# Shared-expert linear factors taken into the last but one half batch, unbroken last subtractions, and biases behind the last span chain, in a perceiver layer

## Chip, cores and metric

The kernel runs on one core of one Trainium2 chip, as one launch. The metric is the device time in microseconds (us) of one execution; lower is better. All arithmetic is float32.

## What is computed

There are 32 batches of 64 tokens with 256 features, and a context of 1601 rows of 256 features for each batch. Three residual steps follow each other, each on a layer norm of x:

```python
# 1. cross-attention, 16 heads of 16
q, k, v = split(ln(x) @ wq.T + bq), split(ctx @ wk.T + bk), split(ctx @ wv.T + bv)
x = x + merge(softmax(q @ k.T / 4, mask) @ v) @ wo.T + bo
# 2. span attention among the 64 tokens: two numbers per head and token
span = heads(ln(x) @ W_span.T)
mean, soft = sigmoid(span[..., 0]) * 64, softplus(span[..., 1])
x = x + merge(softmax(-soft * (pos - mean)**2) @ heads(ln(x) @ W_val.T)) @ W_out.T
# 3. feed-forward: one shared expert, and two of eight experts chosen by the token's index
xf = ln(x)
shared = (silu(xf @ sw1 + sb1) * (xf @ sw3 + sb3)) @ sw2 + sb2
routed = sum(gelu(xf @ w1[e] + b1[e]) @ w2[e] + b2[e] for e in two_experts(token)) / 2
x = x + (shared + routed) / 2
```

## The kernel before

**Engines.** PE is TensorE, DVE VectorE, ACT ScalarE, POOL GpSimd; SP issues nearly all loads and stores. PE, DVE, ACT and POOL run their instructions in the order in which the program writes them between `order.enter_context` (L629) and `order.close()` (L749). Outside that stretch, and for SP's loads and stores throughout, a planner puts the instructions in order by the times that it estimates. PE's results lie in PSUM; six banks of 128 x 512 are shared by most matmuls of the attention part (`mm_bank`, L94), and a bank is used again when its reader is done.

**Half batches.** `halves` (L388) has 64 entries: batch b, and c for the first or last eight heads. The work of half batch n is written in four groups of key blocks (`GROUPS`, L33). While half batch n is normalised, the scores of n+1 are made: `scores` (L461, matmul L469) with the mask added by DVE (L478), running maxima on DVE (L499) begun by a copy on ACT (`first_maxima`, L490). Maxima are turned (L506), reduced (L513), spread over rows (L521) and copied (L525). `less_maxima` (L528) subtracts them from four pairs of heads, on POOL for n < 63 and on DVE for the last n (all at L530); `exponentials` (L534, L535) is ACT's. `values` (L537, L545) multiplies with v. In between, PE projects the keys and values of the next batch (L434, L450); for the last batch there is no next one, so half batches 62 and 63 have none of that.

**Steps between the groups.** Each half batch has four stretches, 4n to 4n+3. `agenda` (L595) holds generators by stretch and `run` (L597) lets each take a step, written into the order at that place. `finish_steps` (L603) ends a batch: a copy (L608), a matmul (L611), a reciprocal (L615) and a product (L618). After every second batch `span_steps` (L206) follows for a tile of 128 tokens, some 17 stretches long: output projection (L210), residual (L213), statistics, L184 on POOL (a power, for the norm's scale), L190 and L191, turn (L198), copy (L220), span matmul (L224) and values (L236), copy of the span (L229) on DVE and of the values (L242) on ACT, absolute value (L250) and exponential (L251) on ACT, a run of small DVE operations (L265 to L281), then on [128, 16, 64]: POOL subtracts (L286), ACT squares (L290), POOL scales (L291), DVE finds the least (L294), POOL subtracts (L295), ACT exponentiates (L297), DVE sums (L299) and inverts (L300), POOL scales (L301); PE turns (L309), ACT copies (L311), PE multiplies (L319), ACT copies (L325), PE multiplies (L329), DVE adds (L332), SP stores the tile to `x_kept` (L334), and after another norm and turn DVE copies it to `xfT` (L340). There are 16 tiles; tile 14 is under way in half batches 60 to 63, tile 15 after the last half batch.

**Shared expert.** Its first layer is cut into 16 units: four quarters of the tokens by four chunks of 128 hidden features. `unit(u)` makes both products (L575) in two PSUM banks; `gate()` applies Silu with its bias on ACT (L590) and adds the other bias and multiplies on DVE (L591). Quarter 3, units 12 to 15, needs tile 15. The results lie in parts of `prob`, the tile of the probabilities, that are free by then (`region`, L558). Units 0 to 2 are made and gated in half batch 62, unit 3 is made and gated and unit 4 made in half batch 63, the others while the last tile's span steps run, by the two tables `begin` (L737) and `gated` (L738), and quarter 3 at the end.

**Experts.** After `order.close()` come the weight loads (L761), the load of the second biases (L773), the doubling of `sw2` on POOL (L775), the biases of the eight classes of tokens on POOL (L780, L784, L787), and for each class a load of its rows of `x_kept` (L796) to which POOL adds the bias (L797). Then for each of eight classes PE makes two experts' hidden layers (L808), ACT applies gelu (L815), PE sums shared and routed outputs (L826), DVE scales and adds the rows (L828) and SP stores (L829).

Of the kernel before, what the change touches and what calls it, by code (L numbers as in the profile page):

```python
# [15 lines left out]
F32 = mybir.dt.float32  # L16
U8 = mybir.dt.uint8
AF = mybir.ActivationFunctionType
# [4 lines left out]
P = 128  # L23
# [53 lines left out]
def perceiver_kernel(ctx: ExitStack, tc: tile.TileContext, a: dict[str, bass.AP], out: bass.AP):  # L77
# [83 lines left out]

    neghalf = const.tile([P, 1], F32, name="neghalf")
# [43 lines left out]
    def span_steps(t: int, oT):  # L206
# [21 lines left out]
        span = span_pool.tile([P, H, 2], F32, tag="span", name=f"span_{t}")  # L228
        nc.vector.tensor_copy(span.rearrange("p h k -> p (h k)"), psp[:, : 2 * H])  # L229

# [18 lines left out]
        z = span_pool.tile([P, H, 2], F32, tag="z", name=f"z_{t}")  # L249
        nc.scalar.activation(z, span, AF.Abs)  # L250
# [315 lines left out]
    waiting: deque = deque()  # L566

    def unit(u: int):
        quarter, hc = divmod(u, NHC)
        slot = slice(quarter * QL, (quarter + 1) * QL)  # L570
        pair = []
        for name, w in (("p1", sw1), ("p3", sw3)):
            ps = mm_bank(f"{name}_{u}")
            for c in range(2):
                nc.tensor.matmul(  # L575
                    ps, lhsT=w[:, c, hc * P : (hc + 1) * P], rhs=xfT[:, c, :, slot],
                    start=(c == 0), stop=(c == 1),
                )
            pair.append(ps)
        waiting.append((u, *pair))  # L580

    def gate():
        u, p1, p3 = waiting.popleft()
        quarter, hc = divmod(u, NHC)
        act = gated_at(1, 2)
        if u > 2:
            act = spare[:, 0, (4 + u % 2) * E * QL : (5 + u % 2) * E * QL]
            act = act.rearrange("p (r i) -> p r i", r=E)
        p1, p3 = (ps.rearrange("p (r i) -> p r i", r=E) for ps in (p1, p3))
        nc.scalar.activation(act, p1, AF.Silu, bias=cols[:, B_S1 + hc : B_S1 + hc + 1])  # L590
        nc.vector.scalar_tensor_tensor(  # L591
            gated_at(quarter, hc), p3, cols[:, B_S3 + hc : B_S3 + hc + 1], act, ALU.add, ALU.mult
        )
# [67 lines left out]
    for n, (b, c) in enumerate(halves):  # L661
# [12 lines left out]
        for g in range(len(GROUPS)):  # L674
            if waiting and n < last:
                gate()
            if g == 0:
                turned = []
                if n < last:

                    def turn():
                        turned.extend(turned_maxima(n))
                        return turned

                    scores(n + 1, g, BETWEEN[g], turn)
                else:
                    turned = turned_maxima(n)
                    maxima_of_rows(*turned)
            elif n < last:
                scores(n + 1, g, BETWEEN[g])  # L690
            if g == 0:
                project(project_keys, c, 0)
                m = maxima_along_rows(turned[1])
                if n == last:
                    unit(3)
# [6 lines left out]
            elif g == 1:  # L702
                project(project_keys, c, 1)
                project(project_values, 3 * c)
            elif g == 2:
                project(project_keys, c, 2)
                if c:
                    project(project_values, 4)
            else:
                project(project_keys, c, 3)  # L710
                for u in range(5 if c else 1, 7 if c else 3):
                    project(project_values, u)

            less_maxima(n, g, m, nc.vector if n == last else nc.gpsimd)
            run(4 * n + g)
            if n == last - 1 and g < 3:
                unit(g)
            if n == last and g == 1:
                gate()
                unit(4)  # L720
            if g == 0 and n < last:
                first_maxima(n + 1)
            if g:
                exponentials(n, g - 1)
        if n < last:
            for k in BETWEEN[-1]:
                maximum(n + 1, k)
    exponentials(last, 3)
    values(last, 0)
    values(last, 1)  # L730
    stretch = 4 * last + 4
    finish = finish_steps(B - 1, stretch)
    next(finish)
    agenda[stretch].append(finish)


    begin = {1: 5, 4: 6, 7: 7, 9: 8, 10: 9, 12: 10, 16: 11}  # L737
    gated = {1: 1, 4: 1, 7: 1, 9: 1, 10: 1, 12: 1, 14: 1}  # L738
    for s in range(19):
        run(stretch + s)  # L740
        for _ in range(gated.get(s, 0)):
            gate()
        if s in begin:
            unit(begin[s])
# [3 lines left out]
    gate()  # L748
    order.close()  # L749
# [22 lines left out]
    b2row = ffn.tile([P, E + 1, D], F32, name="b2row")  # L772
    nc.sync.dma_start(out=b2row, in_=a["b2"].partition_broadcast(P))  # L773

    nc.gpsimd.tensor_tensor(sw2, sw2, sw2, ALU.add)  # L775


    brow = spare[:, 2, 4 * D : (4 + E) * D].rearrange("p (r d) -> p r d", r=E)
    for r in range(E):
        nc.gpsimd.tensor_tensor(  # L780
            brow[:, r, :], b2row[:, expert_of(0, r), :], b2row[:, expert_of(1, r), :], ALU.add
        )
    for _ in range(2):
        nc.gpsimd.tensor_tensor(  # L784
# [112 lines left out]
```

## Time and profile before

| what | value |
|---|---|
| median of 3 runs | 1655.0 us (1652.92 to 1655.36) |
| profiled execution, its own time | 1654.66 us |
| its span, first to last instruction | 1652.9 us |
| mean granted TensorE clock | 0.993 |
| PE busy (share of the span) | 1572.0 us (95%) |
| weight loads on PE busy | 1182.3 us (72%) |
| DVE busy | 1288.4 us (78%) |
| ACT busy | 921.0 us (56%) |
| POOL busy | 1120.8 us (68%) |

The page's second part cuts the span into 40 slices of 41 us. PE stands at nine tenths in nearly all; two slices near the end show 7 and 6, and there the granted clock (PEclk) has its one 7. Most of the program is the same pattern repeated 64 times, which the change doesn't touch but for one small operation per tile; what it does touch lies between 1449.8 us, where half batch 62 begins, and 1566 us, where the routed experts begin. The timeline (instructions in order of time) and the chain of waits (the work that ended last) over that window, and a table of busy times by stretches, are the views to read. In the timeline each row has the start, the duration, the engine, the line and what it writes from what; a number in brackets is the idle time of the engine just before, with what ended it.

### The profile page before, as it was taken

How to read it: one execution, taken by the hardware profiler on the slowest of the kernel's cores; microseconds unless marked ns; L12 is line 12 of the kernel's file. 1: busy time of each engine (PE TensorE's matmuls, PEld its weight loads, DVE VectorE, ACT ScalarE, POOL GpSimd, SP SyncE). 2: the span in 40 equal slices, each digit the busy share in tenths (PEclk: the TensorE clock that was granted, in tenths of full speed). 3: DMA queues.
4: the chain of work that ended last, by engine and by line, in shares of the span. 5: the costliest groups of instructions: out<-in, count | busy, mean ns of one | idle time of the engine just before them, and what ended most of it. 6: DMA issues, size and time to landing. Idle time of an engine off the chain costs nothing.

```text
span 1652.9 us, 55724 instructions
## 1 busy us (share of the span) xinstructions
PE 1572.0 (95%) x25128; PEld 1182.3 (72%) x25128; DVE 1288.4 (78%) x2619; ACT 921.0 (56%) x1279; POOL 1120.8 (68%) x410
## 2 busy tenths in 40 slices
PE   8999999999999999999999999999999999979699
PEld 5777777777777777777777777777777777745388
DVE  4888988888888978888888889888888889785100
ACT  3555656556656556565665656565666565566211
POOL 0777767777686867687686877677776869653600
PEclk9999999999999999999999999999999999999799
DMA  5111111111111111111111111111111111003100
GB/s 174 54 41 30 42 40 33 39 42 49 42 42 48 29 40 34 41 39 48 42 42 49 42 36 36 39 40 39 42 48 42 42 45 30 31 15 109 55 23 29
DMA packets 52045, 73.67 MB, mean 45 GB/s; under 512 B 3812, under 2 KB 51040, under 8 KB 51680
## 3 DMA queue, kind: packets, MB, share of 16 engines
q1 hardware_dynamic: 50992, 69.32, 14.4%
q8 instruction: 197, 3.23, 0.8%
q10 hardware_dynamic: 816, 0.79, 0.1%
q14 instruction: 40, 0.33, 0.1%
HBM read 65.90 MB, written 4.19 MB: 42 GB/s over the span
## 4 chain that ended last, share of the span: by engine, by line
PE 57%; DVE 38%; issue 2%; POOL 1%; ACT 1%; DMA 0%; ACTq 0%; DVEq 0%; POOLq 0%
DVE prob L478 13%; DVE mrun L499 13%; PE pk L434 13%; PE pv L450 13%; PE pvs L545 9%; PE psc L469 8%; PE py L826 3%; DVE rin L615 3%; PE p L575 2%; PE pm L506 2%; PE ph L808 2%; PE pb L521 1%; DVE mrun L279 1%; DVE least L294 1%; PE pval L236 1%
## 5 line engine op out<-in xcount | busy, mean ns | idle before, releaser
L530 POOL TENSOR_TENSOR prob<-prob,mb 124x1664 f32<-124x1664 f32 x252 | 935.3, 3730 | 326.7 <-ACT mb L525 326.7
L478 DVE TENSOR_TENSOR prob<-psc,madd 124x384 f32<-124x384 f32 (+1 forms) x1024 | 582.1, 581 | 183.4 <-PE psc L469 183.4
L499 DVE TENSOR_TENSOR mrun<-prob,mrun 124x512 f32<-124x512 f32 x704 | 483.1, 686 | 7.2 <-ACT mrun L491 4.3
L434 PE MATMUL pk<-ct,wkT_sb 128*128 128x372 f32 (+2 forms) x1024 | 407.8, 521 | 14.3 <-DMA wkT_sb<-in_wkT 5.6
L535 ACT ACTIVATE prob<-prob 124x1664 f32<-124x1664 f32 x256 | 399.6, 1587 | 1.5 <-POOL prob L530 1.0
L450 PE MATMUL pv<-wvT_sb,ct 128*124 128x256 f32 (+1 forms) x1664 | 384.6, 379 | 0.0
L450 PEld LDWEIGHTS pv<-wvT_sb,ct 128*124 128x124 f32 (+1 forms) x1664 | 309.9, 186 | 77.3 <-DVE prob L478 2.4
L469 PE MATMUL psc<-qbd,kT 32*124 32x128 f32 x6656 | 294.6, 286 | 30.6 <-DVE prob L478 26.0
L438 ACT ACTIVATE kT<-pk,cols 128x372 f32<-128x372 f32 (+2 forms) x256 | 152.1, 594 | 292.4 <-PE pk L434 292.0
L469 PEld LDWEIGHTS psc<-qbd,kT 32*124 32x124 f32 x6656 | 232.5, 181 | 104.3 <-DVE prob L478 48.1
L434 PEld LDWEIGHTS pk<-ct,wkT_sb 128*128 128x128 f32 x1024 | 174.2, 190 | 118.7 <-issue 29.4
L456 ACT COPY v<-pv 124x512 f32<-124x512 f32 (+1 forms) x224 | 124.7, 557 | 215.2 <-PE pv L450 213.8
L545 PE MATMUL pvs<-prob,v 124*17 124x64 f32 x13312 | 211.3, 219 | 1.8 <-ACT prob L535 1.8
L545 PEld LDWEIGHTS pvs<-prob,v 124*17 124x17 f32 x13312 | 188.8, 98 | 27.5 <-issue 25.2
L828 DVE SCALAR_TENSOR_TENSOR ot<-py,prob 128x256 f32<-128x256 f32 x16 | 6.8, 424 | 76.9 <-PE py L826 76.9
L615 DVE RECIPROCAL rin<-pr 128x256 f32<-128x256 f32 x32 | 55.9, 1745 | 6.3 <-PE pr L611 6.3
L575 PE MATMUL p<-xfT,sw_sb 128*128 128x512 f32 x128 | 59.7, 619 | 0.7 <-DVE xfT L340 0.4
L521 PEld LDWEIGHTS pb<-cst,mc 128*124 128x124 f32 x256 | 29.8, 135 | 35.8 <-DVE mc L513 30.1
L506 PE MATMUL pm<-cst,mx 124*128 124x124 f32 x256 | 40.7, 282 | 10.4 <-DVE mx L499 9.4
L575 PEld LDWEIGHTS p<-xfT,sw_sb 128*128 128x128 f32 x128 | 25.0, 200 | 30.1 <-issue 27.1
L499 DVE TENSOR_TENSOR mx<-prob,mrun 124x512 f32<-124x512 f32 x64 | 43.9, 686 | 2.2
L815 ACT ACTIVATE hT<-ph,cols 128x256 f32<-128x256 f32 x32 | 13.4, 471 | 57.4 <-PE ph L808 57.4
(123 smaller groups left out, 1235.0 us busy)
## 6 DMA issues: line engine op xcount, KB each, us to landing
ct<-in_ctxT SPq DMA_DIRECT2D x64, 372.0 KB, 3.2
ct<-in_ctxT SPq DMA_DIRECT2D x32, 496.0 KB, 3.5
ct<-in_ctxT SPq DMA_DIRECT2D x32, 361.0 KB, 3.1
w<-in_w SPq DMA_DIRECT2D x16, 256.0 KB, 4.8
x<-in_x SPq DMA_DIRECT2D x16, 128.0 KB, 2.0
x_kept<-x SPq DMA_DIRECT2D x16, 128.0 KB, 1.7
prob<-x_kept SPq DMA_DIRECT2D x8, 256.0 KB, 6.0
out<-ot SPq DMA_DIRECT2D x16, 128.0 KB, 1.9
```

The costliest lines, as they stand in the source:

```text
L434: nc.tensor.matmul(ps[:, :kn], lhsT=wkT[:, i, c * P : (c + 1) * P], rhs=cts[b][g][:, i, :kn], start=(i == 0), stop=(i == 1),)
L438: nc.scalar.activation(kTs[c][:, k0 : k0 + kn], ps[:, :kn], AF.Identity, bias=cols[:, B_K + c : B_K + c + 1])
L450: nc.tensor.matmul(ps[:kn, n * D : (n + 1) * D], lhsT=cts[b][g][:, i, k0 : k0 + kn], rhs=wvT[:, i, :], start=(i == 0), stop=(i == 1),)
L456: nc.scalar.copy(vs[b % 2][:kn, 2 * u : 2 * u + n, :, :DK], ps[:kn, : n * D].rearrange("p (n h d) -> p n h d", n=n, d=DK),)
L469: nc.tensor.matmul(ps[:CHUNK, k * P : (k + 1) * P], lhsT=kTs[c][32 * j : 32 * j + 32, at : at + CHUNK], rhs=qbd[b // 2][32 * j : 32 * j + ...
L478: nc.vector.tensor_tensor(pair_of(n, j)[:, c0 : c0 + nb, :].rearrange("p k (e q) -> p k e q", e=2), ps[:CHUNK, : nb * P].rearrange("p (k e ...
L499: nc.vector.tensor_tensor(dst, block_of(n, k), run, ALU.max)
L530: engine.tensor_tensor(sj, sj, m[:CHUNK, j, None, :].to_broadcast([CHUNK, NKC, P]), ALU.subtract)
L535: nc.scalar.activation(pair_of(n, j), pair_of(n, j), AF.Exp)
L545: nc.tensor.matmul(pvs[32 * j : 32 * j + DK + 1, c, r, :], lhsT=v[:kn, k, 8 * c + h, :], rhs=pair_of(n, h // 2)[:kn, k, (h % 2) * S : (h % ...
L575: nc.tensor.matmul(ps, lhsT=w[:, c, hc * P : (hc + 1) * P], rhs=xfT[:, c, :, slot], start=(c == 0), stop=(c == 1),)
L615: nc.vector.reciprocal(rin, pr[:, : 4 * S])
```

## The change

The second factor of six units is made ahead of its gate. `half_unit` makes one of the two products. `linear_factor(u)` makes the product with `sw3`, and ACT writes it, with its bias added, to the place of the unit's result; later `unit(u)` makes only the product with `sw1`, and `gate` applies Silu in place in PSUM and multiplies. This is done for units 0, 1, 2, 4, 5 and 6, in the four stretches of half batch 62, where units 0 to 2 were made and gated before.

`sw3` and its bias are doubled at the start of the program (POOL and DVE), instead of `sw2` at the end.

In span_steps the absolute value is made on DVE, right behind the span's copy, from the span and its PSUM bank.

Half batch 63 has code of its own. The four subtractions on DVE and the four exponentials on ACT are written one behind the other; the values, the units and the steps come after. Units and gates have new places in the two tables, which now count from the half batch's first stretch (4 more than before), and two gates stand between the values and the rest.

The biases' work on POOL and the loads that it needs are written at the end of the ordered stretch, behind the last unit, and ahead of the weight loads. It is done class by class, in small operations, and the bias rows lie in `prob`.

```diff
+    nc.gpsimd.tensor_tensor(sw3, sw3, sw3, ALU.add)
+    b3twice = const.tile([P, NHC], F32, name="b3twice")
+    nc.vector.tensor_scalar(b3twice, cols[:, B_S3 : B_S3 + NHC], 2.0, None, ALU.mult)
...
         nc.vector.tensor_copy(span.rearrange("p h k -> p (h k)"), psp[:, : 2 * H])
+        nc.vector.scalar_tensor_tensor(
+            z.rearrange("p h k -> p (h k)"), span.rearrange("p h k -> p (h k)"), -1.0,
+            psp[:, : 2 * H], ALU.mult, ALU.max,
+        )
...
-        nc.scalar.activation(z, span, AF.Abs)
         nc.scalar.activation(z, z, AF.Exp, scale=-1.0)
...
+    def half_unit(u: int, w):
+        quarter, hc = divmod(u, NHC)
+        slot = slice(quarter * QL, (quarter + 1) * QL)
+        ps = mm_bank(f"u{u}")
+        for c in range(2):
+            nc.tensor.matmul(
+                ps, lhsT=w[:, c, hc * P : (hc + 1) * P], rhs=xfT[:, c, :, slot],
+                start=(c == 0), stop=(c == 1),
+            )
+        return ps.rearrange("p (r i) -> p r i", r=E)
+
+    def linear_factor(u: int):
+        quarter, hc = divmod(u, NHC)
+        nc.scalar.activation(
+            gated_at(quarter, hc), half_unit(u, sw3), AF.Identity, bias=b3twice[:, hc : hc + 1]
+        )
+        linear.add(u)
+
+    def unit(u: int):
+        begun.append((u, half_unit(u, sw1), None if u in linear else half_unit(u, sw3)))
...
     def gate():
...
+        if u in linear:
+            nc.scalar.activation(p1, p1, AF.Silu, bias=bias)
+            nc.vector.tensor_tensor(at, p1, at, ALU.mult)
+        else:
...
+            nc.scalar.activation(act, p1, AF.Silu, bias=bias)
+            nc.vector.scalar_tensor_tensor(at, p3, b3twice[:, hc : hc + 1], act, ALU.add, ALU.mult)
...
+    extra = {4 * last - 4: (0,), 4 * last - 3: (1, 2), 4 * last - 2: (4, 5), 4 * last - 1: (6,)}
+    for n, (b, c) in enumerate(halves[:-1]):
...
             less_maxima(n, g, m, nc.gpsimd)
             run(4 * n + g)
+            for u in extra.get(4 * n + g, ()):
+                linear_factor(u)
...
+    stretch = 4 * last
+    values(last - 1, 0)
+    exponentials(last - 1, 3)
+    turned = turned_maxima(last)
+    maxima_of_rows(*turned)
+    m = maxima_along_rows(turned[1])
+    for j in range(4):
+        less_maxima(last, j, m, nc.vector)
+        exponentials(last, j)
+    values(last - 1, 1)
+    unit(3)
+    run(stretch)
     values(last, 0)
+    unit(0)
+    run(stretch + 1)
     values(last, 1)
+    finish = finish_steps(B - 1, stretch + 4)
     next(finish)
+    agenda[stretch + 4].append(finish)
+    gate()
+    gate()
...
-    begin = {1: 5, 4: 6, 7: 7, 9: 8, 10: 9, 12: 10, 16: 11}
-    gated = {1: 1, 4: 1, 7: 1, 9: 1, 10: 1, 12: 1, 14: 1}
-    for s in range(19):
+    begin = {4: (1,), 5: (2, 4), 8: (7, 8, 5), 11: (9,), 13: (10,), 16: (6,), 20: (11,)}
+    gated = {5: 1, 8: 2, 11: 2, 13: 1, 14: 1, 16: 1, 18: 1}
+    for s in range(2, 23):
...
+    b2row = spare[:, 2, 4 * D : (4 + E + 1) * D].rearrange("p (e d) -> p e d", d=D)
+    nc.sync.dma_start(out=b2row, in_=a["b2"].partition_broadcast(P))
+    shared_twice, *brows = (spare[:, i, 12 * D : 13 * D] for i in (4, 0, 3))
+    nc.gpsimd.tensor_tensor(shared_twice, b2row[:, E, :], b2row[:, E, :], ALU.add)
+    xe = []
+    for r in range(E):
...
+        nc.sync.dma_start(out=xe[r], in_=kept_rows[r])
+        brow = brows[r % 2]
+        nc.gpsimd.tensor_tensor(
+            brow, b2row[:, expert_of(0, r), :], b2row[:, expert_of(1, r), :], ALU.add
+        )
+        nc.gpsimd.tensor_tensor(brow, brow, shared_twice, ALU.add)
+        nc.gpsimd.tensor_scalar(brow, brow, 0.25, None, ALU.mult)
+        nc.gpsimd.tensor_tensor(
+            xe[r], xe[r], brow[:, None, :].to_broadcast([P, 2, D]), ALU.add
+        )
     order.close()
...
-    nc.gpsimd.tensor_tensor(sw2, sw2, sw2, ALU.add)
```

## The prediction

> **What bounds the kernel now.** The page's chain of work (part 4) gives PE 57% and DVE 38% of 1652.9 us. The change rewrites the end of the program, so I read the chain and the timeline from half batch 62 on (the last but one; it begins at 1449.8 us) and ask at each step what ended last. Four places carry the prediction.
>
> First, POOL alone in the timeline of the tail (start, duration, line, what ended the idle time before it):
>
> ```profile
> 1522.25 2.78 POOL L780 TENSOR_TENSOR prob<-b2row 128x256 f32<-128x256 f32 x4
> 1524.99 1.90 POOL L295 TENSOR_TENSOR sc<-sc,least 128x1024 f32<-128x1024 f32 x1
> 1526.85 2.78 POOL L780 TENSOR_TENSOR prob<-b2row 128x256 f32<-128x256 f32 x4
> 1529.70 9.07 POOL L784 TENSOR_TENSOR prob<-prob,b2row 128x2048 f32<-128x2048 f32 x2
> 1538.73 1.90 POOL L301 TENSOR_TENSOR sc<-sc,total 128x1024 f32<-128x1024 f32 x1
> ```
>
> L295 and L301 belong to the last chain, L780 and L784 are the biases. L295's input (L294) is there at 1523.55, it starts at 1524.99: 1.44 late. L301's input (L300) is there at 1529.52, it starts at 1538.73: 9.21 late. Who waits is PE:
>
> ```profile
> 1540.68 1.97 PE L309 MATMUL psa<-cst,sc 128*128 128x128 f32 x8 [11.48 <-POOL sc L301]
> ```
>
> Second, the clock that PE then gets. In the table by stretches (PEclk is the seventh value):
>
> ```profile
> 1476.00:1480.00 4.00, 0.00 (x0) 0.00 (x0) 3.97 (x7) 1.43 (x1) 1.21 (x1) 1.00 0.00 0
> 1480.00:1487.00 7.00, 5.41 (x13) 3.00 (x14) 3.96 (x5) 1.54 (x2) 0.69 (x1) 0.51 0.00 0
> 1541.00:1547.00 6.00, 5.42 (x45) 3.93 (x44) 1.17 (x2) 2.14 (x4) 4.97 (x1) 0.50 0.01 3
> ```
>
> After each long PE idle (1475.6 to 1480.8, and 1529.2 to 1540.7) six to seven us run at half clock: eight L309 take 1.97 here, 1.04 at 1493.88.
>
> Third, half batch 62 is DVE's: no projections are left, and DVE stands in order behind a gate whose Silu waits for a table load:
>
> ```profile
> 1459.69 0.59 ACT L491 COPY mrun<-prob 124x512 f32<-124x512 f32 x1 [2.46 <-DVE soft L281]
> 1460.30 1.28 ACT L590 ACT_TABLE_LOAD   x1
> ...
> 1461.60 0.69 ACT L590 ACTIVATE prob<-p,cols 128x512 f32<-128x512 f32 x1
> 1462.30 1.28 ACT L535 ACT_TABLE_LOAD   x1
> 1462.32 0.75 DVE L591 SCALAR_TENSOR_TENSOR prob<-p,cols,prob 128x512 f32<-128x512 f32 x1 [2.71 <-ACT prob L590]
> ```
>
> Fourth, the last half batch: subtractions and exponentials are broken up by the gate of unit 3, its table loads and L299, L300.
>
> ```profile
> 1484.45 3.69 DVE L530 TENSOR_TENSOR prob<-prob,mb 124x1664 f32<-124x1664 f32 x2 [1.82 <-ACT mb L525]
> ...
> 1490.05 5.10 DVE L530 TENSOR_TENSOR prob<-prob,mb 124x1664 f32<-124x1664 f32 x2
> ...
> 1495.48 3.08 ACT L535 ACTIVATE prob<-prob 124x1664 f32<-124x1664 f32 x2
> ```
>
> Two subtractions alone take 3.69; the other pair takes 5.10, with POOL's L301 beside it.
>
> **Half batch 62.** PE's work is equal: three whole units of 3.45 go, six halves of 1.72 come. From DVE go three L591 (0.75, about 0.66 apart) and the 2.71 wait, from ACT three Silu and six loads of 1.28 (two per gate, three gates). ACT gains six Identity evictions. The trace has none; the nearest row is L590, the same 128x512 from PSUM with a bias column: 0.69 (bounds: L525's copy 0.58, L591's 0.75). I take 0.69, 4.1 in all, in time that the loads held. The first one waits for PE till about 1458.5 and is over before DVE's L281 ends (1459.61), so L491 behind it is not late; the pair before the third score group stands behind L290, which needs POOL's L286 (1465.15), and gives its banks back about 1468.7.
>
> DVE from L281's end at 1459.61: three score groups of 3.66 (1462.98 to 1466.64), L615 with L618 2.12, L294 1.12, three maxima 2.06, 0.2 for L491: 16.5, so 1476.1. For a score group that waits for the evictions' banks I add 0.4 (bounds 0 and 0.9, the time of 24 score matmuls). The last maximum ends at 1476.5 instead of 1480.77: 4.3. PE is then idle some 3.0 us rather than 5.2. L506 and L521 took 1.1 each at half clock, 0.64 and 0.62 at 1452.43 and 1454.60: another 1.0 if the clock holds. "TensorE: Matmul & The Clock Gate", Part 1, puts the drop after an idle window of about 3.4 us. The rows agree with a limit between 1.2 (before 1498.61, no drop) and 4.4 us, but don't place it; by the rule 3.0 is short enough and the 1.0 is mine, by a limit below 3 it is lost. I take it: 5.3.
>
> A rule against the change: "ScalarE: Activation LUTs", Rules for kernel authors, gives additions to VectorE. The rows price the same tile at 0.69 on ACT and 0.75 on DVE, and here DVE is the engine that others wait for: by the rows the exchange costs 4.1 of idle ACT, by the rule it would be a loss for DVE's sake. The same page's What ACT_TABLE_LOAD costs says 2.66 us per switch with its drain. The rows show 1.28 with 0.02 before it; by the page six switches would be 16 us of ACT, by the rows 7.7. I use the rows.
>
> **The last half batch, to L615.** Let T be the end of L525 (1484.42 before). Four unbroken L530 are 7.4, the last L535 1.58: T+9.0. Now L297 (1.06), which stood ahead, is behind the exponentials on ACT; then L299 1.2, L300 0.25, L301 1.9, L309 1.04, and PE reaches the matmul of L611 only behind L309: 0.6, with hand-overs T+15.2. That is a new wait, and without it values would be done at T+10.7. The two gates written ahead of L615 on DVE are over at T+14.5 (o copy, load 1.28, two Silu, two products), so they hide. Before, L615 began at T+17.03: 1.8 gained.
>
> **L615 to the last span matmul.** Before: 1501.45 to 1510.81, 9.37. The chain's links are equal, but L198 of the last tile stands behind half units 2 and 4 (3.45) that stand behind L329: PE gets to it 8.75 after L615 instead of 8.06. 0.7 lost.
>
> **Span matmul to L309.** Before 29.87. Less 1.44 and 9.21. The absolute value moves to DVE (L229's 0.18 is the nearest row; bounds 0.1 and 0.41, L213's) and ACT's 0.23 goes, but two Silu instead of one stand ahead of the exponential's table load: 0.5 lost. 19.7. PE's filling there is 1.0 plus units 7, 8, 9, 10 and halves 5, 6: 18.3 to 18.9, just under it, so PE's idle time goes from 11.5 to about 0.8, and the clock holds. Gain 10.2.
>
> **L309 to the last four units.** Before 1540.68 to 1551.54, 10.86 at half clock. At full clock: L309 1.04, copy 0.6, L319 0.5, copy 0.45, L329 1.1, unit 11 3.45, L198 and L340 0.6: 7.8 with hand-overs. Gain 3.0. The four units (14.0) and the routed experts (83) are PE's in order and stay.
>
> **Equal answers.** Other tiles' 15 extra DVE operations (0.18 each) hide in DVE's wait for scores behind L229 (0.79 at 1257.96); uncovered they cost 2.7. The biases' work on POOL is 0.7 + 8 x (2 x 0.69 + 0.67 + 1.24), from L780, L787, L797: 27 us behind the last L184 (about 1529). The first output needs its part only 29 us after L184 (1548.0 to 1577.2), then one each 10.36, against 3.3 of POOL: hidden, also with 4 us of load ahead. On SP the eight row loads and b2row are now written ahead of the weights; if the twelve weight loads (7 us of issue) really waited for them, the next ones are wanted over 20 us after L184. The doubling of sw2 (1.89) leaves POOL between two L184, worth nothing; that of sw3 moves to the start, where POOL is idle from 8.5 to 33.6, with a small DVE multiply in an idle gap: zero if POOL takes L184 first.
>
> **Sum:** 5.3 + 1.8 - 0.7 + 10.2 + 3.0 = 19.6. I take off 0.6 for bank waits I can't see: 19.0. The profiled execution took 1654.66 around its span of 1652.9, the median is 1655.0: 1636.0.
>
> **Rivals.**
> (a) PE becomes the bound behind the chain. If unit 7 gets banks only when gates 2 and 4 are done, PE starts 2.3 later and L309 comes 1.5 late; if two idle spells of about 2.5 (before L309, before unit 7) drop the clock, each costs half of 7 us. Gain 11 to 15: 1640 to 1644. For it: 18.3 against 19.7 is tight. Against: six banks, and four are held there. 0.17.
> (b) POOL takes the doubling of sw3 ahead of L184 at the start. That load is issued at 11.9 and lands 7.1 later: 19.0 plus 1.9, against L184 at 7.99; with it everything is 12.9 late: 1649. Against: DVE's early operations of before stand mixed by the arrival of their loads, not as written. 0.05.
> (c) Slower: the same place, but the memsets behind it too (1.5) and a later landing; it turns the sign once sw3 lands 5 us later than in the trace (24 instead of 19), and at 26 gives about 1658. 0.03.
> (d) The gain is given back: every stretch of the tail is held by PE's units in order, so that the 10.65 taken from POOL becomes waiting for PE. The units that fill are 17.2 before and after, and PE was idle 11.5 there, so this asks for misplacement throughout; about 1654. 0.02.
> My case has 0.73, its own range is 1632.5 to 1639.5. With most of (a): 1632.5 to 1643. Faster by over 0.2% (about what a measurement of this kernel can tell): 0.95; within 0.2%: 0.02; slower: 0.03.
>
> **What would show it.** L301 of the last tile right behind L300; PE's wait before the last L309 under 2 us and PEclk at 1.0 from there; no ACT_TABLE_LOAD in half batch 62, last maximum there near 1476.5; four L530 in 7.4; L611 behind L309; the four last units beginning near 1532.5; no wait of L828 for POOL. Wrong if PE's clock is at half before L506 or between L210 and L309 of the last tile, or if the first scores begin later than 16 us.

## The result and the profile after

The changed kernel takes 1636.07 us (median of 4 runs, 1635.48 to 1639.21); the kernel before, run beside it, takes 1655.18 us (1652.92 to 1656.44). The ratio is 0.989, with a 95% interval of 0.9873 to 0.9907. The predicted time was 1636.0. The profiled execution of after took 1636.38 us with a span of 1634.6, so both spans and own times are 18.3 apart between the two profiles.

In the changed kernel the lines have other numbers: L295 and L301 (POOL, last chain) are now L303 and L309, L309 (PE turns) is L317, L506 and L521 (maxima turned and spread) are L514 and L529, L530 (subtractions) is L538, L297 (the span's exponential) is L305, L615 (the reciprocal) is L632, the gate that only multiplies is L604 with L605, the whole gate L609 with L610, and L590 is the new eviction. T stays the end of the copy of the maxima (L525 before, L533 after).

First POOL's timeline in the tail of after (start, duration, engine, line):

```profile
1518.73 1.90 POOL L303 TENSOR_TENSOR sc<-sc,least 128x1024 f32<-128x1024 f32 x1 [1.33 <-DVE least L302]
1523.41 1.90 POOL L309 TENSOR_TENSOR sc<-sc,total 128x1024 f32<-128x1024 f32 x1 [2.77 <-DVE total L308]
1530.70 0.55 POOL L189 TENSOR_TENSOR rstd_f<-ve_f,neghalf 128x1 f32<-128x1 f32 x1 [5.40 <-DVE ve_f L187]
1531.22 0.61 POOL L775 TENSOR_TENSOR prob<-prob 128x256 f32<-128x256 f32 x1
...
1533.40 0.86 POOL L786 TENSOR_SCALAR prob<-prob 128x256 f32<-128x256 f32 x1
```

POOL now waits for DVE ahead of L303 and L309; the releasers end where they start. The biases begin at 1531.22, behind the last norm. Then PE's timeline, at the maxima and at the last chain:

```profile
1476.65 0.61 PE L514 MATMUL pm<-cst,mx 124*128 124x124 f32 x4 [3.36 <-DVE mx L507]
1478.04 1.11 PE L529 MATMUL pb<-cst,mc 128*124 128x128 f32 x4 [0.77 <-DVE mc L521]
...
1525.36 1.09 PE L317 MATMUL psa<-cst,sc 128*128 128x128 f32 x8 [1.48 <-POOL sc L309]
```

The wait of 11.48 for POOL is 1.48, and these eight take 1.09 instead of 1.97. But of the two small groups at the maxima the first runs at full speed and the second at half. The table by stretches says the same (the stretch and its length, then the busy time of PE, PEld, DVE, ACT and POOL; the value behind these is the granted clock):

```profile
1473.84:1477.25 3.41, 0.59 (x4) 0.41 (x4) 2.60 (x4) 1.68 (x2) 2.83 (x2) 1.00 0.00 0
1479.00:1484.00 5.00, 5.00 (x108) 3.70 (x108) 4.14 (x3) 2.59 (x3) 0.00 (x0) 0.50 0.02 5
1525.00:1534.00 9.00, 7.47 (x56) 4.37 (x57) 3.01 (x9) 3.59 (x7) 3.44 (x6) 1.00 0.21 63
```

The clock is held behind the last chain. At the maxima it is lost at 1477.25 and back at 1484.08. ACT's timeline in half batch 62, and at the end:

```profile
1459.17 0.69 ACT L590 ACTIVATE prob<-u,b3twice 128x512 f32<-128x512 f32 x1 [1.57 <-PE u L582]
1460.00 0.59 ACT L499 COPY mrun<-prob 124x512 f32<-124x512 f32 x1
...
1488.69 1.04 ACT L305 ACTIVATE sc<-sc 128x1024 f32<-128x1024 f32 x1
1491.84 0.37 ACT L625 COPY o<-pvs 128x256 f32<-128x256 f32 x1 [2.12 <-PE pvs L553]
1492.23 1.28 ACT L609 ACT_TABLE_LOAD   x1
```

Between 1450.5 and the end of the exponentials no table is loaded. The first load stands behind the o copy. DVE's timeline in the last half batch:

```profile
1479.86 7.30 DVE L538 TENSOR_TENSOR prob<-prob,mb 124x1664 f32<-124x1664 f32 x4 [1.88 <-ACT mb L533]
...
1494.25 0.75 DVE L610 SCALAR_TENSOR_TENSOR prob<-u,b3twice,prob 128x512 f32<-128x512 f32 x1 [2.98 <-ACT prob L609]
1494.92 0.68 DVE L605 TENSOR_TENSOR prob<-u,prob 128x512 f32<-128x512 f32 x1
1495.51 1.75 DVE L632 RECIPROCAL rin<-pr 128x256 f32<-128x256 f32 x1
```

Four unbroken subtractions take 7.30. L632 stands right behind the second gate: the gates hold it, not PE (L628, its input, is done at 1494.90).

The prediction cut the tail into stages that follow each other. Measured from the two profiles:

| stage | before | after | gained | predicted |
|---|---|---|---|---|
| to T | 1484.42 | 1479.82 | 4.60 | 5.3 |
| T to the reciprocal (L615, L632) | 17.03 | 15.69 | 1.34 | 1.8 |
| to the end of the last span matmul | 9.37 | 9.97 | -0.60 | -0.7 |
| to L309, now L317 | 29.87 | 19.88 | 9.99 | 10.2 |
| to the last four units (1551.54, 1533.27) | 10.86 | 7.91 | 2.95 | 3.0 |
| sum | | | 18.3 | 19.6, less 0.6 |

From the last four units to the end it takes 101.3 in both.

### The profile page after: what moved, and what is told of

It reads as the page before. It is cut to its first block, busy times and chain, and to the rows that moved or that the text cites. A ratio compares the mean times of both kernels' runs of the same rounds, so it can differ in the third digit from the quotient of the medians.

```text
span 1634.6 us, 55734 instructions
## 1 busy us (share of the span) xinstructions
PE 1568.6 (96%) x25128; PEld 1181.3 (72%) x25128; DVE 1290.9 (79%) x2636; ACT 910.2 (56%) x1261; POOL 1119.9 (69%) x424
## 4 chain that ended last, share of the span: by engine, by line
PE 57%; DVE 39%; issue 2%; ACT 1%; POOL 0%; DMA 0%; ACTq 0%; DVEq 0%; POOLq 0%
DVE prob L486 13%; DVE mrun L507 13%; PE pk L442 13%; PE pv L458 13%; PE pvs L553 10%; PE psc L477 8%; PE py L838 3%; DVE rin L632 3%; PE pm L514 2%; PE u L582 2%; PE ph L820 2%; PE pb L529 1%; DVE least L302 1%; DVE mrun L287 1%; DVE total L307 1%
## 5 line engine op out<-in xcount | busy, mean ns | idle before, releaser
L538 POOL TENSOR_TENSOR prob<-prob,mb 124x1664 f32<-124x1664 f32 x252 | 935.4, 3730 | 326.6 <-ACT mb L533 319.8
L553 PE MATMUL pvs<-prob,v 124*17 124x64 f32 x13312 | 212.3, 220 | 0.0
L553 PEld LDWEIGHTS pvs<-prob,v 124*17 124x17 f32 x13312 | 189.9, 98 | 26.9 <-issue 26.1
L840 DVE SCALAR_TENSOR_TENSOR ot<-py,prob 128x256 f32<-128x256 f32 x16 | 6.8, 425 | 76.9 <-PE py L838 66.1
L582 PE MATMUL u<-xfT,sw_sb 128*128 128x512 f32 x128 | 58.6, 608 | 0.5 <-DVE xfT L348 0.4
L632 DVE RECIPROCAL rin<-pr 128x256 f32<-128x256 f32 x32 | 56.0, 1749 | 0.3 <-PE pr L628 0.3
L529 PEld LDWEIGHTS pb<-cst,mc 128*124 128x124 f32 x256 | 29.8, 135 | 35.8 <-DVE mc L521 30.0
L514 PE MATMUL pm<-cst,mx 124*128 124x124 f32 x256 | 40.3, 280 | 8.5 <-DVE mx L507 7.5
L582 PEld LDWEIGHTS u<-xfT,sw_sb 128*128 128x128 f32 x128 | 24.2, 194 | 27.8 <-issue 24.8
```

Source lines behind the costliest of these rows:

```text
L538: engine.tensor_tensor(sj, sj, m[:CHUNK, j, None, :].to_broadcast([CHUNK, NKC, P]), ALU.subtract)
L553: nc.tensor.matmul(pvs[32 * j : 32 * j + DK + 1, c, r, :], lhsT=v[:kn, k, 8 * c + h, :], rhs=pair_of(n, h // 2)[:kn, k, (h % 2) * S : (h % ...
L582: nc.tensor.matmul(ps, lhsT=w[:, c, hc * P : (hc + 1) * P], rhs=xfT[:, c, :, slot], start=(c == 0), stop=(c == 1),)
L632: nc.vector.reciprocal(rin, pr[:, : 4 * S])
```

## The experiments

My theory: the time before was set by POOL's place in the last chain (a little over two thirds), the rest by DVE behind the gates of half batch 62, and PE's clock goes with both. The rivals: (R1) the biases' place alone would have brought nearly all, since a faster half batch 62 only makes PE wait elsewhere; (R2) the clock, not the waiting, is what the linear factors pay, so that a PE that is kept fed at the maxima would gain more; (R3) the eviction could as well be VectorE's; (R4) the last half batch is held by its gates and by L317 that stands ahead of L628.

| run | median us (lowest to highest) | ratio to before, 95% interval |
|---|---|---|
| e1_bias_only | 1641.64 (1641.04 to 1643.10) | 0.9912 (0.9898 to 0.9927) |
| e2_bias_back | 1654.31 (1651.20 to 1655.46) | 0.9989 (0.9982 to 0.9996) |
| e3_units_back | 1646.60 (1644.16 to 1647.17) | 0.9938 (0.9923 to 0.9953) |
| e4_linear_dve | 1639.17 (1638.60 to 1643.56) | 0.9903 (0.9887 to 0.9920) |
| e5_fill | 1636.12 (1633.64 to 1638.44) | 0.9884 (0.9869 to 0.9899) |
| e6_fill_more | 1634.99 (1634.24 to 1637.45) | 0.9880 (0.9863 to 0.9896) |
| e7_span_early | 1632.74 (1631.57 to 1633.14) | 0.9863 (0.9848 to 0.9877) |
| e8_all | 1637.85 (1637.58 to 1638.72) | 0.9896 (0.9881 to 0.9910) |
| e9_fill_span_early | 1632.19 (1631.51 to 1633.76) | 0.9859 (0.9845 to 0.9874) |
| e10_early_gates_later | 1637.19 (1636.04 to 1638.50) | 0.9886 (0.9869 to 0.9902) |

The kernel before, run beside them, had medians of 1655.55 (e1 to e4), 1655.21 (e5 to e8) and 1655.31 (e9, e10). Where I compare with "after", it is with its median of 1636.07.

One difference doesn't come from the edits. In the profiles of before, after, e1 and e2 it takes 101.3 from the last four units to the end; in those of e3 to e10 it takes 100.1. PE's timeline where the first routed expert begins, in after and in e7:

```profile
1548.18 7.17 PE L820 MATMUL ph<-xfT,w 128*128 128x256 f32 x32 [0.91 <-DVE prob L610]
```

```profile
1543.48 7.07 PE L816 MATMUL ph<-xfT,w 128*128 128x256 f32 x32
```

In after PE waits there for the last gate's product, in e3 to e10 it doesn't. This part lies behind `order.close()`, where the planner decides; why it came out differently is not shown. So e3 to e10 have some 1.2 us against after that their edits were not meant to bring. Among themselves they compare without it.

### e1_bias_only: the biases' place alone

The kernel before, with the biases' work and its loads at the end of the ordered stretch, and nothing else of the change.

```diff
+    b2row = spare[:, 2, 4 * D : (4 + E + 1) * D].rearrange("p (e d) -> p e d", d=D)
+    nc.sync.dma_start(out=b2row, in_=a["b2"].partition_broadcast(P))
...
     order.close()
...
-    b2row = ffn.tile([P, E + 1, D], F32, name="b2row")
-    nc.sync.dma_start(out=b2row, in_=a["b2"].partition_broadcast(P))
...
```

> The kernel before with one edit: the biases' work on POOL and its loads stand at the end of the ordered stretch, in the changed kernel's form; sw2 is still doubled on POOL at the end, the units, the order of the last half batch and the absolute value stay. Theory (POOL's order is the largest part): the two delays of the last chain, 1.44 and 9.21, go, PE's idle time before the last psa falls under 1.5 us, the clock holds and the psa-to-last-units stretch takes 7.9 instead of 10.86. Gain 13.6, so 1641.6 us. Rival (d) of the prediction (the gain is given back to waiting for PE's units): 1650 or more. Second rival (the size of the gain comes from the last half batch, not from here): at most 5 us, 1650.

Measured, in POOL's timeline (L295 and L301 have their old numbers here):

```profile
1523.72 1.90 POOL L295 TENSOR_TENSOR sc<-sc,least 128x1024 f32<-128x1024 f32 x1 [1.33 <-DVE least L294]
1528.39 1.90 POOL L301 TENSOR_TENSOR sc<-sc,total 128x1024 f32<-128x1024 f32 x1 [2.77 <-DVE total L300]
1535.69 0.55 POOL L184 TENSOR_TENSOR rstd_f<-ve_f,neghalf 128x1 f32<-128x1 f32 x1 [5.39 <-DVE ve_f L182]
```

Both steps of the chain start right behind DVE, as in after. 13.9 of the gain come from this place alone (1655.55 to 1641.64), as the sum of the prediction has it (10.65 of waiting and 3.0 of clock). R1 is half right: most of it, but 5.6 are left for the rest of the change.

### e2_bias_back: all of the change but the biases' place

The changed kernel with the biases' work behind `order.close()` again, as before.

```diff
-    b2row = spare[:, 2, 4 * D : (4 + E + 1) * D].rearrange("p (e d) -> p e d", d=D)
...
     order.close()
...
+    b2row = ffn.tile([P, E + 1, D], F32, name="b2row")
+    nc.sync.dma_start(out=b2row, in_=a["b2"].partition_broadcast(P))
...
```

> The changed kernel with one edit undone: the biases' work stands behind the ordered stretch again, as before, so that the planner places it on POOL. Its place in POOL's queue differs from that of before: six small sums stand ahead of the span step that scales, two more and the two large additions ahead of the one that subtracts the least, the 5.4 us multiply ahead of the last. From the durations of before: the scaling comes 3.0 late, the subtraction of the least 9.1 more late, the last step 2.8 more; 14.8 in all, and with PE idle that long 2.9 for the half clock. 17.7 slower than the changed kernel: 1653.8 us. If the tail were held by PE instead (the biases have room), it stays within 2 us of the changed kernel, 1636 to 1638.

POOL's timeline of this kernel (L800, L804 and L807 are the biases):

```profile
1514.14 4.15 POOL L800 TENSOR_TENSOR prob<-b2row 128x256 f32<-128x256 f32 x6
1518.25 1.90 POOL L299 TENSOR_TENSOR sc<-sc,soft 128x1024 f32<-128x1024 f32 x1
...
1521.59 9.07 POOL L804 TENSOR_TENSOR prob<-prob,b2row 128x2048 f32<-128x2048 f32 x2
1530.62 1.90 POOL L303 TENSOR_TENSOR sc<-sc,least 128x1024 f32<-128x1024 f32 x1
1532.49 5.37 POOL L807 TENSOR_SCALAR prob<-prob 128x2048 f32<-128x2048 f32 x1
1537.84 1.90 POOL L309 TENSOR_TENSOR sc<-sc,total 128x1024 f32<-128x1024 f32 x1
```

Undoing the place costs 18.2, more than doing it alone brought: with the chain earlier, the planner's order puts biases into three links of it (L299, L303, L309), where before it was two. What the rest of the change gained upstream is eaten by POOL. The parts of the change don't add up, and the loss of an engine in order depends on what it happens to meet.

### e3_units_back: no linear factors

The changed kernel with whole units and gates in half batch 62 again, unit 4 in the last half batch, and the rest of the change kept.

```diff
...
+            if begun:
+                gate()
...
-            for u in extra.get(4 * n + g, ()):
-                linear_factor(u)
+            if n == last - 1 and g < 3:
+                unit(g)
...
-    unit(0)
+    unit(4)
...
-    begin = {4: (1,), 5: (2, 4), 8: (7, 8, 5), 11: (9,), 13: (10,), 16: (6,), 20: (11,)}
-    gated = {5: 1, 8: 2, 11: 2, 13: 1, 14: 1, 16: 1, 18: 1}
+    begin = {5: (5,), 8: (6, 7), 11: (8,), 13: (9,), 16: (10,), 20: (11,)}
+    gated = {8: 1, 11: 2, 13: 1, 14: 1, 18: 1}
```

> The changed kernel without linear factors: units 0 to 2 are made and gated whole in half batch 62 as before, with their six table loads and the order of before; units 4 to 11 are whole and fill the tail in the same amounts of PE time. Theory: the last maximum of half batch 62 ends near 1481 us instead of 1476.5, PE is idle over 5 us before it and the clock drops, so that the maxima's spread is done near 1484.8 instead of 1479.8: 5.0 slower, 1641.1 us, and the rest of the tail is shifted but not longer. Rival (half batch 62 hides its gates and the gain came from the last half batch's order): within 1.5 us of the changed kernel.

It is 10.5 slower than after; I had expected 5. In the profile T comes at 1484.15, 4.3 later, where 5.0 were expected, and the last four units begin 11.2 later. The reciprocal comes at T+17.17 instead of T+15.69, since a whole unit stands on PE between two sets of values (3.70 instead of 1.98). And behind the last chain the clock is lost again. PE's timeline there, and the table by stretches:

```profile
1531.75 1.68 PE L317 MATMUL psa<-cst,sc 128*128 128x128 f32 x8 [2.18 <-POOL sc L309]
1533.35 1.40 PE L327 MATMUL po<-aT,vbd 128*32 128x64 f32 x32
...
1538.23 5.64 PE L582 MATMUL u<-xfT,sw_sb 128*128 128x512 f32 x8
```

```profile
1532.10:1542.34 10.24, 8.54 (x48) 4.91 (x47) 2.00 (x6) 4.87 (x8) 2.36 (x4) 0.50 0.09 29
```

From L317 to the last units it takes 12.72 instead of 7.91. PE was idle for only 2.18 ahead of L317; in e4 and e5 spells of 2.21 and 2.90 ahead of tile 14's L317 left the clock alone. That asked for the experiments on the clock below.

### e4_linear_dve: the eviction on VectorE

The changed kernel, with the eviction as an addition on DVE.

```diff
-        nc.scalar.activation(
-            gated_at(quarter, hc), half_unit(u, sw3), AF.Identity, bias=b3twice[:, hc : hc + 1]
-        )
+        nc.vector.tensor_scalar(
+            gated_at(quarter, hc), half_unit(u, sw3), b3twice[:, hc : hc + 1], None, ALU.add
+        )
```

> The changed kernel, but the six linear factors are evicted by VectorE (a tensor_scalar addition of the bias, PSUM to SBUF, 128x512) instead of ScalarE. Theory: DVE has no gap in half batch 62 once L281 is done, so each costs its 0.66 us there: six are 4.0, 1640.1 us, with the clock dropping as in the changed kernel. By the rule that additions belong to VectorE it would be no slower than ScalarE's eviction: 1636 us.

DVE's timeline in half batch 62 of this kernel:

```profile
1466.28 1.40 DVE L590 TENSOR_SCALAR prob<-u,b3twice 128x512 f32<-128x512 f32 x2
...
1472.51 0.75 DVE L590 TENSOR_SCALAR prob<-u,b3twice 128x512 f32<-128x512 f32 x1 [0.52 <-PE u L582]
...
1480.24 0.69 DVE L507 TENSOR_TENSOR mx<-prob,mrun 124x512 f32<-124x512 f32 x1
```

0.75 on DVE against 0.69 on ACT, and the last maximum ends 4.4 later (1480.93 against 1476.51), which is six times about 0.7. The last four units begin 4.26 later (1537.53); the time shows 3.1 of it, since the 1.2 at the end goes the other way. So R3 falls. The rule that the prediction weighed (the Trainium skill, "ScalarE: Activation LUTs", Rules for kernel authors) gives additions to VectorE and names its speed in bf16 as the reason; for this float32 addition from PSUM it would have lost these 3.1 us. The engine that others wait for should not get the work, whichever is faster at it.

### e5_fill and e6_fill_more: PE kept fed ahead of the maxima

In the prediction the clock would hold if PE's idle spell at the maxima was short enough. e5 moves half unit 0 from the last half batch to the spot just ahead of the turned maxima; e6 makes the linear factor of unit 3 there as well.

```diff
     exponentials(last - 1, 3)
+    linear_factor(3)
+    unit(0)
     turned = turned_maxima(last)
...
     values(last, 0)
-    unit(0)
```

(e5 has only the two lines with `unit(0)`.)

> The changed kernel with unit 0's remaining half (1.7 us of PE) moved from behind the values of half batch 63 to just before the turn of the maxima, into PE's idle 3.4 us. PE is then idle about 1.6 us there instead of 3.4. If any PE work keeps the clock, the clock stays at 1.0 over the turns and the values behind them. If transposes don't count for the clock (the turns of the maxima and their spreading are transposes, and stood alone between 1473.3 and 1479.1), the drop only comes about 1.8 us later, near 1479, and values and unit 3 still run at half clock. In both cases the second set of transposes takes 0.6 instead of 1.1, unit 0 no longer stands between the two sets of values, and L632 begins 1.0 earlier: 1635.1 us, which only the profile can resolve.

PE's timeline of e5:

```profile
1472.30 1.98 PE L582 MATMUL u<-xfT,sw_sb 128*128 128x512 f32 x4
1475.73 0.61 PE L514 MATMUL pm<-cst,mx 124*128 124x124 f32 x4 [1.45 <-DVE mx L507]
1477.11 1.11 PE L529 MATMUL pb<-cst,mc 128*124 128x128 f32 x4 [0.77 <-DVE mc L521]
1478.15 2.65 PE L553 MATMUL pvs<-prob,v 124*17 124x64 f32 x104
```

The idle spell ahead of L514 is 1.45, and still L529 takes 1.11: the clock falls at 1476.91. Neither case of the expectation came. If any work on PE kept the clock it would have stayed; if transposes counted as idle time the fall would have come near 1479, later than in after, and it came earlier. The spell without any matmul but transposes (L514, L529 and L317 all are), from 1474.28 to 1478.15, is 3.87; a second such spell of 3.83 (1489.54 to 1493.37, L317 within) left the clock at 1.00. The four executions differ too: 1633.64 and 1634.24 with a mean granted clock of 0.999, 1638.44 and 1637.99 with 0.997. The first of these is the profiled one.

> As the last one, with the linear factor of unit 3 made there too (another 1.7 us, evicted by ScalarE): PE has non-transpose work until the turn of the maxima, and only 2.3 us lie between it and the next values. By both views of what counts the clock stays at 1.0 throughout. L632 begins 1.0 to 1.2 earlier than in the changed kernel: 1635.0 us.

The table by stretches of e6:

```profile
1473.00:1490.00 17.00, 12.18 (x342) 7.64 (x332) 12.09 (x11) 10.90 (x10) 3.52 (x2) 1.00 0.01 3
1494.00:1498.00 4.00, 4.00 (x38) 2.06 (x37) 2.18 (x2) 0.89 (x3) 0.00 (x0) 0.59 0.91 323
```

Now the clock holds through the maxima (L514 0.59, L529 0.65) and falls 17 us later, behind a spell of 3.82 with only L317 in it. The filling moves the loss rather than ending it: 1.1 faster than after by the medians, with intervals that overlap, and no more than the 1.2 at the end. R2 is not carried by the time.

What drops the clock shows in the lengths of the falls. In the twelve traces of this case, up to the last unit, the clock stands at half for 3.41 us (e5, e6, e7, e9), for 6.83 (before, after, e1), for 10.24 (e3, e8, e10), for 17.07 (before) or for 20.48 (e2): always a whole multiple of 3.41. So is the time at full clock between two falls (44.37 in before, 13 of them). The clock changes only at the steps of a raster of 3.41 us, whose place differs from trace to trace. Laid along it, the table by stretches gives for the two spells of e5, and then for that of e6:

```profile
1473.49:1476.91 3.42, 1.41 (x6) 0.41 (x4) 2.55 (x5) 1.59 (x1) 2.29 (x2) 1.00 0.00 0
1490.56:1493.97 3.41, 1.53 (x14) 1.21 (x18) 1.35 (x2) 2.80 (x5) 1.82 (x1) 1.00 0.86 243
```

```profile
1490.44:1493.85 3.41, 1.09 (x9) 1.10 (x10) 1.50 (x3) 2.78 (x4) 1.90 (x1) 1.00 0.63 192
```

The clock fell at the end of the first and the third, with PE busy for 1.41 and 1.09, and stayed behind the second, with 1.53. The second and the third hold nearly the same spell; the raster only cuts it at another place. This sorts nearly all that there is: in the twelve traces (from 200 us to the last unit) every step at full clock with PE busy for 1.41 or less ended in a fall, 17 in all, and every one with 1.50 or more kept the clock but one (e4, fall at 1467.22, 2.02 busy). The ends of matmuls are modelled, so the limit between 1.41 and 1.50 is an estimate.

Transposes are counted as work in these figures, and without them the steps don't sort: of the 1.53 only 0.61 are other matmuls, and the clock stayed; before lost it at 1531.28 with 1.34 of others and no transposes. The Trainium skill ("TensorE: Matmul & The Clock Gate", Part 1) describes a window of about 3.4 us that runs free of the program; the raster agrees with it. Its Part 4 says that transposes don't count as PE's work in the same way; these traces speak against that.

### e7_span_early: L317 out of the way of the values

The step of tile 14 that holds the exponential L305 (and so L307 to L309) stands ahead of the four subtractions, and the two gates ahead of L632 move behind the finishing step's reciprocal.

```diff
     m = maxima_along_rows(turned[1])
+    run(stretch)
     for j in range(4):
         less_maxima(last, j, m, nc.vector)
...
     unit(3)
-    run(stretch)
...
-    gate()
-    gate()
...
-    gated = {5: 1, 8: 2, 11: 2, 13: 1, 14: 1, 16: 1, 18: 1}
+    gated = {4: 2, 5: 1, 8: 2, 11: 2, 13: 1, 14: 1, 16: 1, 18: 1}
```

> The changed kernel with the new wait of its last half batch taken away: the step that holds tile 14's exponential on ScalarE (L305) is written ahead of the four subtractions and exponentials (ScalarE is idle 1.96 us there), and the two gates behind the last batch's finish step instead of ahead of it. Theory: POOL's last scaling of tile 14 is then done near 1490.7, so that psa and pr follow the values (done at 1491.8) at once, and no gate stands before L632: it begins near 1493.5 instead of 1495.5, and everything behind is 2.0 earlier, 1634.1 us. Rival (something else is as late: the o copy, a bank): under 0.5 us.

PE's timeline of e7, and DVE's:

```profile
1488.79 1.56 PE L553 MATMUL pvs<-prob,v 124*17 124x64 f32 x97
1490.29 1.09 PE L317 MATMUL psa<-cst,sc 128*128 128x128 f32 x8
1491.22 0.60 PE L628 MATMUL pr<-o,cst 128*128 128x256 f32 x2
```

```profile
1491.85 1.76 DVE L632 RECIPROCAL rin<-pr 128x256 f32<-128x256 f32 x1 [3.67 <-PE pr L628]
```

L317 has its input in time and costs PE no wait; the reciprocal stands at 1491.85, T+12.41 instead of T+15.69, released by L628 and not by a gate. Of these 3.28, 1.05 are the clock: it stood at half for 3.41 here and for 6.83 in after, and the second set of values is done at T+10.9 instead of T+12.0. The other 2.2 are the order, where 2.0 were expected. The last four units begin 3.63 earlier (1529.64), so nothing of it is given back on the way. The median is 3.3 below that of after, and 1.2 of this is the wait at the end. R4 is confirmed, with some 2 us.

### e8_all, e10_early_gates_later and e9_fill_span_early: what e8 lost

e8 joins e6's filling and e7's order, and takes the gates of units 2 and 4 one stretch later, behind the absolute value's exponential (L259) on ACT. Only this last edit, against e7's table, is shown.

```diff
-    gated = {4: 2, 5: 1, 8: 2, 11: 2, 13: 1, 14: 1, 16: 1, 18: 1}
+    gated = {4: 2, 5: 1, 9: 2, 11: 2, 13: 1, 14: 1, 16: 1, 18: 1}
```

> The last two together (unit 0's half and unit 3's linear factor before the turn; tile 14's exponential early; the two gates later), and the two gates of units 2 and 4 behind the last tile's first exponential instead of ahead of it, so that its table load doesn't wait for two Silu (1.24). Theory: the maxima's spread 0.5 earlier, L632 12.5 behind it instead of 15.7, 3.7 in all; span matmul to last psa 18.9 (PE's filling) instead of 19.9. 4.6 us less than the changed kernel: 1631.5 us. If PE's units in order are by now the bound, the last 1.0 is lost: 1632.5.

At 1637.85 it is slower than after, where 1631.5 was expected. DVE's timeline of e8:

```profile
1507.69 1.29 DVE L605 TENSOR_TENSOR prob<-u,prob 128x512 f32<-128x512 f32 x2 [4.90 <-ACT u L604]
1508.89 0.17 DVE L273 TENSOR_SCALAR mrun<-z 128x16 f32<-128x16 f32 x1
```

I had moved the Silus off the exponential's way on ACT, and not seen the products: on DVE they stand in order ahead of L273, the start of the chain, and now wait for Silus behind another table load. L273 is 6.56 behind the last span matmul (e7: 4.66), PE idles 3.38 ahead of L317, and the clock falls there. Two runs take e8 apart: e10 has the early step and the later gates without the filling, e9 the filling and the early step with the gates left alone.

> The changed kernel with the last tile's step to L305 ahead of the four subtractions, and the two gates of units 2 and 4 one stretch later, behind the absolute value's exponential; no filling ahead of the maxima. If these gates alone cost e8_all its time: L273 6.5 behind the span matmul, TensorE idle over 3 us ahead of psa, half clock behind it, 1636 to 1638. If the filling had to be there too: within 1 us of the run with the earlier step alone, 1632 to 1634.

DVE's timeline of e10:

```profile
1508.42 1.29 DVE L605 TENSOR_TENSOR prob<-u,prob 128x512 f32<-128x512 f32 x2 [4.90 <-ACT u L604]
1509.63 0.17 DVE L273 TENSOR_SCALAR mrun<-z 128x16 f32<-128x16 f32 x1
```

> The changed kernel with the filling of TensorE ahead of the turned maxima (unit 0's half and the linear factor of unit 3) and the last tile's step to L305 ahead of the four subtractions, the gates of units 2 and 4 left where the changed kernel has them. If the gates moved behind the exponential's stretch were what cost e8_all its time (L273 6.6 us behind the span matmul, then an idle TensorE of 3.4 us and a clock at half), L273 is 4.7 behind the span matmul again, psa stands about 1522, the last units begin near 1529.5 and the time is 1632 to 1633. If it was the filling together with the earlier step, the time stays at 1636 to 1638 and the clock is at half behind psa here too.

PE's timeline of e9:

```profile
1484.79 2.95 PE L553 MATMUL pvs<-prob,v 124*17 124x64 f32 x104 [1.51 <-ACT prob L543]
...
1521.67 1.09 PE L317 MATMUL psa<-cst,sc 128*128 128x128 f32 x8 [1.48 <-POOL sc L309]
```

Both came out as expected: the later gates alone cost 4.5 (e10 against e7), and without them the joined version is the fastest run, 1632.19. Against e7 it gains 0.55, which their ranges don't resolve: here too the clock held at the maxima (L529 takes 0.65) and fell a little later, at 1484.88 behind a step with PE busy for 1.18 (104 matmuls of values take 2.95 at 1484.79; at full speed 1.65).

## Why the prediction came out right

Right in time and in the main steps, with two terms mis-sized, for which the 0.6 taken off made up in part.

- **POOL (10.2, measured 9.99) and the clock behind it (3.0, measured 2.95).** Right: L309 stands right behind L308, PE waits 1.48, PEclk is 1.00. e1 and e2 show that this place carries it.
- **Half batch 62 (4.3, measured 4.26).** Right: the eviction taken from the row of L590 is 0.69 in the trace as well, and the last maximum ends at 1476.51 against 1476.5 worked out. That the two agree to the hundredth is luck: the half batch began 0.35 later than before (L553 at 1450.12, L545 at 1449.77), and the 0.4 added for the evictions' banks did not come. e4 shows that ACT's idle time was the cover.
- **The clock at the maxima (1.0).** This step failed: "by the rule 3.0 is short enough and the 1.0 is mine". PE idled 3.36, and the step of the raster that ended at 1477.25 lay within this spell but for L514, with PE busy for 0.59. L514 was still at full speed, L529 not: T came 3.31 behind the last maximum, 3.65 before, so 0.34 of the 1.0 came. The length of an idle spell is not what decides, and the trace of before already had it: there the clock fell 4.49 after PE went idle at 1475.59, but only 2.08 after it went idle at 1529.20, at the end of a step of which 1.34 was still work:

```profile
1527.86:1531.28 3.42, 1.34 (x4) 0.28 (x2) 2.22 (x3) 2.09 (x3) 3.34 (x4) 1.00 0.00 0
```

So the limit "between 1.2 (before 1498.61, no drop) and 4.4 us" that the prediction sought in the idle time could not be placed by any row. e5 shows the failure with an idle spell of only 1.45.
- **T to the reciprocal (1.8, measured 1.34).** The wait for L317 came as predicted: L628 ended at T+15.1, against T+15.2. But "so they hide" of the gates failed by 0.6: at half clock the values were done at 1491.78, the o copy and the table load stand behind them on ACT, and the second gate let the reciprocal begin at T+15.69; it was to be over at T+14.5. e7 takes both waits away at once, and they were worth 2.2.
- **The reciprocal to the span matmul (-0.7, measured -0.60).** Right.
- **The 0.6 taken off** for bank waits met other misses, by luck: 0.7 and 0.46 of the two terms above. The forecast of 19.0 stood 0.7 above the profiled 18.3. That the median fell by 19.1, a tenth from the forecast, is the luck of 1655.18 and 1636.07: executions of one kernel spread over 3 to 4 us.

**The rivals.** (a) PE did not become the bound: 1.48 of wait are left ahead of L317. But its clock part is real elsewhere: in e3, e8 and e10 the clock fell around an idle spell of 2.2 to 3.4 ahead of L317, and from there to the last units took some 4 us more. (b) and (c): POOL's first L189 starts at 8.21 and the doubling of `sw3` stands at 19.45, so neither came. (The sign that the prediction gave for them, first scores later than 16 us, was too tight: they begin at 16.02 before and at 16.13 after.) (d): nothing was given back, e1 and e3 show that both halves of the change pay. No wait of L840 (L828 before) for POOL was added either. A row of DVE's timeline seems to say otherwise:

```profile
1558.93 0.42 DVE L840 SCALAR_TENSOR_TENSOR ot<-py,prob 128x256 f32<-128x256 f32 x1 [10.80 <-POOL prob L782]
```

But PE's product for it (L838) ends at 1558.81, 0.12 ahead; before, L828 followed its product by 0.11, with the same 10.80 of idle time. L782 at that moment is the eighth class's first step, the first class's part was done at 1535.6 (all eight take 30.8 on POOL, where 27 were worked out, and stay hidden): the name in the brackets is only that of the event nearest to the start.

**What stays open.** Why e4 lost the clock at 1467.22, behind a step with PE busy for 2.02. Whether a transpose counts in full; the traces only show that leaving it out doesn't sort the steps. Where the raster will lie in an execution, which no run here could set. And why the planner spared e3 to e10 the wait ahead of the routed experts.

## What to carry to other kernels

Before work is put on an engine in order, list what stands behind it on that engine and who waits for that: POOL's biases cost 13.9 us there for work that was wanted 29 us behind that chain, and a gate moved to clear ACT cost 4.5 through its product on DVE. Give work to the engine that nobody waits for, even where another does it as fast. Don't judge the clock by the longest idle spell: ask of every stretch of 3.41 us, wherever it may begin, whether PE is busy for at least 1.5 of it. Where some are and some are not, the loss depends on where the raster falls; e5's executions of one program lay 4 us apart. And where an edit lets the planner place something anew, compare the stages behind the edit too: here 1.2 us came from there.

## What the hardware showed unexpectedly

- TensorE's clock fell and came back only on a raster of 3.41 us, and 17 of its 18 falls came at the end of a step in which PE was busy for 1.41 or less, also where no idle spell was longer than 1.51 (e9). A fall lasted from 3.41 (e5) to 20.48 us (e2).
- One program may lose it for a longer or a shorter time: e5's four executions had mean clocks of 0.999, with the one fall of 3.41 in the profiled one, and of 0.997, about three times that loss, and lay 4 us apart.
- On POOL a multiplication of 128x2048 by a constant takes 5.37, an addition of two tiles of that size 4.5 (9.07 for two); at 128x256 it is 0.86 against 0.72.
